# Windowed linear attention behind three convolutions: masks that read a copy of the scores, and norms and divisions set some steps apart

## The chip, the core and the metric

The kernel runs on one core of a Trainium2 chip. Its engines work beside each other, each in the order of its own queue: TensorE (PE), VectorE (DVE), ScalarE (ACT), GpSimd (POOL), and SyncE (SP), which issues most transfers. They wait for each other on semaphores. The metric is the device time of one execution in microseconds; less is better.

## The reference

Four layers act on x of shape 4 x 256 x 48 x 48 in float32. Each adds the result of its block, fed with a group-normalised x, to x:

```python
x = x + L0(_gn(x))   # 7x7 dilated convolution, softmax over 49 taps, applied to x
x = x + L1(_gn(x))   # 3x3 convolution, signs of weights
x = x + L2(_gn(x))   # 3x3 convolution, ternary weights
x = x + L3(_gn(x))   # attention, below
```

The change lies in layer 3 alone. It has 8 heads of 32 channels and three square windows, of the height divided by 1, 2 and 4:

```python
q, k = sigmoid(Wq x), sigmoid(Wk x);  v = Wv x / norm(Wv x)
for w in (1, 2, 4):
    wkv = box sum of k v^T over the window of side H // w around each pixel
    wk  = box sum of k over the same window
    attn = (q . wkv) / (q . wk + 1e-6)
out = Wout concat(attn of the three windows) + bout
```

A window is cut off at the edges of the image. The box sum is linear, so q . wkv is the sum over all pixels in the window of (q . k) v; the kernel computes it so.

## The kernel before

Layers 0 to 2 come first, image by image, and end near 1770 us of the profile. What follows is layer 3.

**Blocks and steps.** A block is one image b, one half ct of the channels (4 heads), and one band rb of 8 query rows: 4 x 2 x 6 = 48 blocks in that order. Inside it the loop runs over key tiles (a, c): 8 rows (band a) by 16 columns (c = 0, 1, 2), which are 128 keys and fill the partitions. `tiles_of` lists the key tiles that the widest window (half side 24) reaches, the nearest bands mixed with the farther ones. That makes 720 steps in all. In a step two pairs of heads are worked on, so that there are 1440 score tiles.

**One step**, in the order of the code:

- `scores`: for each of the two pairs, two matmuls of PE (L1159) write q . k for 128 keys and up to 8 x 48 queries into a PSUM tile `s`. Pool `ps_s` holds two of them, one for each pair, so PE can write the scores of the next step only when those of this step have been read.
- `masked`: the score tile is multiplied by the 0/1 mask of each window into SBUF tiles `sm0`, `sm1`, `sm2` (windows of half side 24, 12 and 6), of which six each are held, three steps' worth.
- `sums`: matmuls (L1237) multiply the masked scores of two steps ago (`LAG = 2`) by v and add them up in three PSUM accumulators.
- `background`: at most one job of other work.

**The masks before.** For a near tile (a band at most two from the queries' band, 1152 of the score tiles) the widest window covers all rows and the middle columns f0 to f1 fully. ACT copies that middle to `sm0` (L1193). DVE multiplies the remaining columns, one or two edges, from PSUM into `sm0`, and the whole of window 1 from PSUM into `sm1` (both L1216). For the nearest bands, at most one away, POOL[...] multiplies window 2 from ACT's copy into `sm2` (L1213, 768 of them). For a far tile (288) DVE multiplies the whole tile from PSUM. A score tile is thus read by ACT and by DVE before PE may write it again.

**Background.** `late` holds jobs with the step at which they are due; if none is due, the next job of `soon` runs. `soon` holds the projections of the next image (q, k, v, and the running sums of k for the box sums, whose rows POOL adds, L952), and the norms q . wk of each band. `norms` yields seven jobs: loads, POOL's subtraction (L1052) and product (L1056) for either half of the channels, `contract` (PE, L1063, sums over a head's channels) and `invert` (DVE). When the second half of a band is done, `finish` puts four jobs into `late`, 1, 4, 8 and 10 steps on: two divisions, of which each loads the reciprocal norms `rc` (L1286, four transfers) and multiplies (DVE, L1292), the first also loading the other half `o` and the residual `res`, and two output projections (PE, L1298).

**Who sets the order.** The matmuls of PE are kept in program order. For the other instructions a scheduler may move one ahead of another on its queue, within their dependencies.

Of the kernel before, what the change touches and what calls it, by code (L numbers as in the profile page):

```python
# [10 lines left out]
F32 = mybir.dt.float32  # L11
# [8 lines left out]
P = 128  # L20
# [4 lines left out]
RB = 8  # L25
# [93 lines left out]
def conv_preact_kernel(  # L119
# [692 lines left out]
    with (  # L812
# [199 lines left out]
        def norms(b, rb):  # L1012


            t = {}

            def load(ct):
                chans = slice(ct * P, (ct + 1) * P)
                t[ct] = hi = scr.tile([P, NW, RB, W], F32, tag="nhi", name="nhi")
                t["lo"] = lo = scr.tile([P, NW, RB, W], F32, tag="nlo", name="nlo", bufs=1)  # L1020
                t["q"] = qf = scr.tile([P, RB, W], F32, tag="nq", name="nq", bufs=1)
                nc.sync.dma_start(
                    out=qf.rearrange("p r w -> p (r w)"),
                    in_=qf_d[b][chans, rb * NB : (rb + 1) * NB],
                )
                for wi, h in enumerate(HALVES):

                    y0 = rb * RB + h - 1
                    n = max(0, min(RB, H - y0))
                    if n > 0:  # L1030
                        nc.sync.dma_start(
                            out=hi[:, wi, 0:n], in_=kb_d[b][wi, chans, y0 : y0 + n, :]
                        )
                    if n < RB:
                        nc.sync.dma_start(
                            out=hi[:, wi, n:RB],
                            in_=kb_d[b][wi, chans, H - 1 : H, :].to_broadcast([P, RB - n, W]),
                        )

                    y0 = rb * RB - h - 1  # L1040
                    n = min(RB, max(0, -y0))
                    if n < RB:
                        nc.sync.dma_start(
                            out=lo[:, wi, n:RB], in_=kb_d[b][wi, chans, y0 + n : y0 + RB, :]
                        )

            def subtract(ct):
                for wi, h in enumerate(HALVES):
                    n = min(RB, max(0, h + 1 - rb * RB))
                    if n < RB:  # L1050
                        hi = t[ct][:, wi, n:RB]
                        nc.gpsimd.tensor_sub(hi, hi, t["lo"][:, wi, n:RB])  # L1052

            def multiply(ct):
                for wi in range(NW):
                    nc.gpsimd.tensor_mul(t[ct][:, wi], t[ct][:, wi], t["q"])  # L1056

            def contract():
                ps = ps_m.tile([P, 512], F32, tag="st", name="norm_ps")
                for ct in range(NCT):  # L1060
                    for wi in range(NW):
                        tc.keep_in_program_order(
                            nc.tensor.matmul(  # L1063
                                ps[D * wi : D * (wi + 1), 0:NB],
                                head_sel[:, ct, :],
                                t[ct][:, wi].rearrange("p r w -> p (r w)"),
                                start=(ct == 0),
                                stop=(ct == NCT - 1),
                            )
                        )  # L1070
                ns = scr.tile([D * NW, NB], F32, tag="ns", name="ns", bufs=1)
                nc.scalar.copy(ns, ps[0 : D * NW, 0:NB])
                for wi in range(NW):
                    nc.sync.dma_start(
                        out=n_d[b][rb, :, wi, :], in_=ns[D * wi : D * wi + HEADS]
                    )

            def invert():
                nn = HEADS * NW * NB // P
                nr = scr.tile([P, nn], F32, tag="nr", name="nr")  # L1080
                flat = [d[b][rb].rearrange("h w n -> (h w n)") for d in (n_d, r_d)]
                nc.sync.dma_start(out=nr, in_=flat[0].rearrange("(p n) -> p n", n=nn))
                nc.vector.tensor_scalar_add(nr, nr, ATTN_EPS)
                nc.vector.reciprocal(nr, nr)
                nc.sync.dma_start(out=flat[1].rearrange("(p n) -> p n", n=nn), in_=nr)

            def between():
                multiply(0)
                load(1)

            return [
                lambda: load(0),
                lambda: subtract(0),
                between,
                lambda: subtract(1),
                lambda: multiply(1),
                contract,
                invert,
            ]
# [29 lines left out]
        def rows_seen(wi, a, rb):  # L1129

            h = HALVES[wi]
            return (
                max(0, a * RB - h + 1 - rb * RB),
                min(RB, a * RB + RB + h - rb * RB),
            )
# [5 lines left out]
        class Block:  # L1141
# [29 lines left out]
            def masked(self, a, c, s):  # L1171

                rb = self.rb
                sr, sc = rows_seen(0, a, rb)[0], cols_seen(0, c)[0]
                res = {}
                copied = None
                for wi in (0, 1, 2):
                    if not seen(wi, a, rb):
                        continue
                    r0, r1 = rows_seen(wi, a, rb)  # L1180
                    c0, c1 = cols_seen(wi, c)
                    n = r1 - r0
                    h = HALVES[wi]
                    sm = smp.tile(
                        [P, 2, RB, min(W, KC + 2 * h)], F32, tag=f"sm{wi}", name=f"sm{wi}"
                    )
                    res[wi] = sm[:, :, 0:n, 0 : c1 - c0]
                    mr = rb * RB + r0 - (a * RB - h + 1)
                    pieces = [(c0, c1)]
                    if wi == 0 and abs(a - rb) * RB + RB <= h:  # L1190

                        f0, f1 = max(0, c * KC + KC - h), min(W, c * KC + h + 1)
                        nc.scalar.copy(  # L1193
                            sm[:, :, 0:n, f0 - c0 : f1 - c0],
                            s[:, :, r0 - sr : r1 - sr, f0 - sc : f1 - sc],
                        )
                        copied = sm, r0, c0, f0, f1
                        pieces = [(c0, f0), (f1, c1)]
                    for p0, p1 in pieces:
                        if p0 == p1:  # L1200
                            continue
                        dst = sm[:, :, 0:n, p0 - c0 : p1 - c0]
                        mc = p0 - (c * KC - MCOL0[wi])
                        m = (
                            mask[wi][:, mr : mr + n, mc : mc + p1 - p0]
                            .unsqueeze(1)
                            .to_broadcast([P, 2, n, p1 - p0])
                        )
                        if wi == NW - 1 and copied and copied[3] <= p0 and p1 <= copied[4]:

                            big, br, bc = copied[:3]
                            src = big[:, :, r0 - br : r1 - br, p0 - bc : p1 - bc]
                            nc.gpsimd.tensor_mul(dst, src, m)  # L1213
                        else:
                            src = s[:, :, r0 - sr : r1 - sr, p0 - sc : p1 - sc]
                            nc.vector.tensor_mul(dst, src, m)  # L1216
                return res

            def begin(self):
                self.accs = [  # L1220
# [47 lines left out]
        def finish(b, rb, stage):  # L1268
# [1 line left out]

            t = {1: stage}

            def divide(ct):
                if ct == 0:
                    t[0] = op.tile([P, NW, NB], F32, tag="o", name="o", bufs=1)
                    nc.sync.dma_start(out=t[0].rearrange("p w n -> p (w n)"), in_=o_d[b][rb])
# [4 lines left out]
                            "(ct p) r w -> p ct r w", p=P  # L1281
                        ),
                    )
                rc = op.tile([P, NW, NB], F32, tag="rc", name="rc", bufs=1)
                for g in range(HG):
                    nc.sync.dma_start(  # L1286
                        out=rc[g * D : (g + 1) * D].rearrange("p w n -> p (w n)"),
# [1 line left out]
                        .rearrange("w n -> (w n)")  # L1289
                        .partition_broadcast(D),  # L1290
                    )
                nc.vector.tensor_mul(t[ct], t[ct], rc)  # L1292

            def out_proj(mo):
                ps = ps_m.tile([P, 512], F32, tag="st", name="out_ps")[:, 0:NB]
# [20 lines left out]
                    )  # L1316

            return [
                lambda: divide(0),
                lambda: divide(1),  # L1320
                lambda: out_proj(0),
                lambda: out_proj(1),
# [45 lines left out]
        def done(i):  # L1368

            b, ct, rb = order[i]  # L1370
            block = blocks.pop(i)
            if ct == 0:
                nc.sync.dma_start(out=o_d[b][rb], in_=block.stage.rearrange("p w n -> p (w n)"))
            else:
                for n, job in zip((1, 4, 8, 10), finish(b, rb, block.stage)):
                    late.append((step + n, job))
            nb, nct = b + (ct + 1) // NCT, (ct + 1) % NCT
            if nb < B:
                for a in LOADS.get(rb, ()):
                    while projected[nb] <= a:  # L1380
                        next_job()
                    load_kv(nb, nct, a)
# [72 lines left out]
```

## Time and profile before

| what | value |
|---|---|
| median of 3 runs (lowest, highest) | 4208.48 us (4205.66, 4213.35) |
| the profiled execution | 4190.68 us, span of its instructions 4188.9 us |
| PE, DVE busy in the span | 3524.6 us, 2265.2 us |
| ACT, POOL busy in the span | 985.1 us, 1217.2 us |
| layer 3 in the span | from about 1770 us to the end, 2419 us |
| masks of DVE, L1216 | 1256.5 us in 2976 instructions |
| window-2 masks of POOL, L1213 | 619.1 us in 768 |
| copies of ACT, L1193 | 598.3 us in 1152 |

A group of instructions is read so: line, engine, operation, tiles written <- tiles read, shape, count | busy time in us, mean ns of one | idle time of the engine just before them, and what ended it. Where a group mixes shapes, a view by form gives each shape its own row. A row of the waits reads: who waited <- for whom: us in all, times, longest.

### The profile page before, as it was taken

The page shows a single profiled execution, that of the slowest core. Times are in us where ns is not written, and L with a number is a line of the kernel's source. Part 1 is how long each engine was busy: PE and PEld are TensorE (multiplying, and loading weights), DVE is VectorE, ACT ScalarE, POOL GpSimd, SP SyncE. Part 2 cuts the span into 40 slices and gives each one's busy share as a digit, 9 for nine tenths or more (in the row PEclk, how much of TensorE's full clock was granted, in tenths as well). Part 3 has the DMA queues.
Part 4 walks back from the last instruction along what each step waited for, and adds up shares of the span by engine and source line. Part 5 has one row for each costly group of instructions (what it writes and reads, how often), then busy time and mean ns, then how long its engine had stood idle before and what let it go on. Part 6 is the DMA issues. An engine that isn't in the chain of part 4 may idle for free.

```text
span 4188.9 us, 65475 instructions
## 1 busy us (share of the span) xinstructions
PE 3524.6 (84%) x25060; PEld 2237.7 (53%) x25060; DVE 2265.2 (54%) x5022; ACT 985.1 (24%) x1915; POOL 1217.2 (29%) x1712
## 2 busy tenths in 40 slices
PE   5999998999899696388888878788978778988888
PEld 4777786787769574134444444434444434444444
DVE  7643234324331225356776667656667656667665
ACT  0101001100110202233332234323234323233332
POOL 0000000010000013465555345562245562223322
PEclk9999999999999798699999999999999999999999
DMA  7333015112500405654455454462353362331321
GB/s 272 131 58 71 23 72 65 42 36 81 72 27 32 37 1 193 177 138 137 150 166 144 114 158 135 126 159 80 93 165 129 124 159 76 93 107 48 93 65 54
DMA packets 366136, 430.06 MB, mean 103 GB/s; under 512 B 141667, under 2 KB 328835, under 8 KB 363395
## 3 DMA queue, kind: packets, MB, share of 16 engines
q1 hardware_dynamic: 360163, 416.37, 36.3%
q10 hardware_dynamic: 5520, 8.00, 0.6%
q8 instruction: 201, 3.29, 0.3%
q0 software_dynamic: 144, 1.52, 0.2%
q14 instruction: 108, 0.88, 0.1%
HBM read 293.12 MB, written 134.17 MB: 102 GB/s over the span
## 4 chain that ended last, share of the span: by engine, by line
PE 57%; DVE 14%; POOL 10%; DMA 9%; issue 4%; ACT 3%; SPq 2%; DVEq 0%; ACTq 0%; POOLq 0%
PE cv L504 15%; PE cv L639 11%; PE acc L1237 11%; PE s L1159 9%; DVE sm L1216 8%; PE out_ps L1298 5%; POOL pt L952 4%; ACT sm L1193 2%; PE proj_ps L898 2%; POOL nhi L1056 2%; PE ap L616 2%; DMA band_d<-e 1%; POOL nhi L1052 1%; POOL sm L1213 1%; DMA ks<-k_d 1%
## 5 line engine op out<-in xcount | busy, mean ns | idle before, releaser
L1216 DVE TENSOR_TENSOR sm<-s,masks 128x128 f32<-128x128 f32 (+14 forms) x2976 | 1256.5, 477 | 506.1 <-ACT sm L1193 487.5
L1159 PE MATMUL s<-qs,ks 128*128 128x320 f32 (+3 forms) x2880 | 798.4, 375 | 361.6 <-DVE sm L1216 257.2
L1213 POOL TENSOR_TENSOR sm<-sm,masks 128x336 f32<-128x336 f32 (+8 forms) x768 | 619.1, 821 | 1148.2 <-ACT sm L1193 1145.0
L1237 PE MATMUL acc<-sm,vs 128*32 128x384 f32 (+18 forms) x13440 | 894.7, 392 | 4.6 <-POOL sm L1213 4.6
L1193 ACT COPY sm<-s 128x528 f32<-128x528 f32 (+2 forms) x1152 | 598.3, 535 | 1196.9 <-PE s L1159 1047.5
L1159 PEld LDWEIGHTS s<-qs,ks 128*128 128x128 f32 x2880 | 460.8, 196 | 768.4 <-issue 449.4
L504 PE MATMUL cv<-v,wt 128*128 128x288 f32 x2912 | 761.9, 416 | 30.5 <-DVE v L460 21.6
L504 PEld LDWEIGHTS cv<-v,wt 128*128 128x128 f32 x2912 | 546.3, 191 | 195.7 <-issue 20.7
L1237 PEld LDWEIGHTS acc<-sm,vs 128*32 128x32 f32 x13440 | 358.4, 112 | 370.9 <-issue 229.7
L639 PE MATMUL cv<-pad,wl_sb 128*128 128x384 f32 (+1 forms) x2592 | 473.6, 345 | 17.1 <-ACT pad L710 12.1
L639 PEld LDWEIGHTS cv<-pad,wl_sb 128*128 128x128 f32 x1728 | 322.1, 193 | 17.6 <-issue 12.4
L448 POOL MEMSET v<- 128x192 f32 x28 | 8.3, 297 | 789.2 <-issue 422.4
L518 DVE SCALAR_TENSOR_TENSOR rows<-cv,rows 128x288 f32<-128x288 f32 x144 | 57.1, 451 | 284.2 <-PE cv L504 284.2
L952 POOL TENSOR_TENSOR pt<-pt 128x144 f32<-128x144 f32 x336 | 190.4, 567 | 59.5 <-DVE pt L948 36.6
L1056 POOL TENSOR_TENSOR nhi<-nhi,nq 128x384 f32<-128x384 f32 x144 | 146.6, 1022 | 21.4 <-DMA nhi<-kb_d 7.3
L672 DVE SCALAR_TENSOR_TENSOR x<-cv,alpha,x 128x384 f32<-128x384 f32 x48 | 29.7, 618 | 224.1 <-PE cv L639 224.0
L1298 PE MATMUL out_ps<-stage,wout_sb 128*128 128x384 f32 x288 | 121.9, 506 | 24.7 <-DVE stage L1292 24.7
L170 ACT ACTIVATE rsq_s<-gn_v 128x2 f32<-128x2 f32 x16 | 3.3, 204 | 557.7 <-DVE gn_v L197 557.6
L1298 PE MATMUL out_ps<-o,wout_sb 128*128 128x384 f32 x288 | 124.2, 514 | 10.0 <-ACT kp L920 5.7
L1307 DVE SCALAR_TENSOR_TENSOR res<-out_ps,bout_sb,res 128x384 f32<-128x384 f32 x48 | 29.7, 618 | 171.7 <-PE out_ps L1298 169.0
L972 PE MATMUL proj_ps<-wv_sb,xn 128*128 128x256 f32 x288 | 98.2, 472 | 25.8 <-ACT kp L920 13.5
L639 PEld LDWEIGHTS <-wl_sb 128*128 128x128 bf16 x864 | 84.8, 99 | 63.1 <-issue 4.4
(160 smaller groups left out, 2654.0 us busy)
## 6 DMA issues: line engine op xcount, KB each, us to landing
qs<-q_d SPq DMA_DIRECT2D x192, 192.0 KB
ks<-k_d SPq DMA_DIRECT2D x192, 192.0 KB
wt<-wt SPq DMA_DIRECT2D x80, 448.0 KB
kb_d<-pt SPq DMA_DIRECT2D x48, 576.0 KB
rc<-r_d SPq DMA_DIRECT2D x192, 144.0 KB
nhi<-kb_d SPq DMA_DIRECT2D x120, 192.0 KB
q_d<-hl SPq DMA_DIRECT2D x48, 384.0 KB
k_d<-hl SPq DMA_DIRECT2D x48, 384.0 KB
```

The lines of the kernel that those rows point to most:

```text
L504: nc.tensor.matmul(pss[half], wt[:, ct, k, :], vt[:, ct, :, t0 : t0 + NTH, k : k + HP], start=((part, ct, k) == (0, 0, 0)), stop=((part, c ...
L616: nc.tensor.matmul(pf[:, f, a:e], xTs[k + i][:n, f, mo * P : (mo + 1) * P], seen[:n, 1 + i, a:e], start=(i == 0), stop=(i == near[-1]),)
L639: nc.tensor.matmul(ps, w_sb[:, ct, t, mo * P : (mo + 1) * P], pad[:, ct, r0 : r0 + RB, c0 : c0 + W], start=(n == 0), stop=(n == len(parts) ...
L952: nc.gpsimd.tensor_add(pt[:, :, r, :], pt[:, :, r, :], up)
L972: nc.tensor.matmul(ps, xn[:, ct, c, :], proj["v"][:, ct, :], start=(ct == 0), stop=(ct == NCT - 1),)
L1056: nc.gpsimd.tensor_mul(t[ct][:, wi], t[ct][:, wi], t["q"])
L1159: nc.tensor.matmul(s[:, j, 0 : (r1 - r0) * (c1 - c0)], kvs[self.b, self.ct, a][0][:, 2 * pr + j, c, :], self.qs[:, 2 * pr + j, r0:r1, c0:c ...
L1193: nc.scalar.copy(sm[:, :, 0:n, f0 - c0 : f1 - c0], s[:, :, r0 - sr : r1 - sr, f0 - sc : f1 - sc],)
L1213: nc.gpsimd.tensor_mul(dst, src, m)
L1216: nc.vector.tensor_mul(dst, src, m)
L1237: nc.tensor.matmul(acc[D * j : D * (j + 1)].rearrange("p (r w) -> p r w", w=W)[:, r0:r1, c0:c1], kvs[self.b, self.ct, a][1][:, c, j, :], s ...
L1298: nc.tensor.matmul(ps, wout_sb[:, kt, mo * P : (mo + 1) * P], t[kt % NCT][:, kt // NCT, :], start=(kt == 0), stop=(kt == NW * NCT - 1),)
```

## The change

ACT copies the whole score tile of a near tile into `sm0`, 640 or 768 elements for each partition in place of 384, 400 or 528. POOL's window 2 and DVE's window 1 are multiplied from that copy, and then DVE multiplies the edges of `sm0` in place. The far tiles stay as they are. Two empty jobs stand between the last product of `norms` and `contract`. `finish` is cut into five jobs, at steps 1, 3, 5, 8 and 10: the loads come two steps ahead of the multiplication that needs them.

```diff
@@ norms
                 lambda: multiply(1),
+                lambda: None,
+                lambda: None,
                 contract,
@@ masked (the new body; tiles, view and times_mask only name slices)
-                    if wi == 0 and abs(a - rb) * RB + RB <= h:
-                        f0, f1 = max(0, c * KC + KC - h), min(W, c * KC + h + 1)
-                        nc.scalar.copy(
-                            sm[:, :, 0:n, f0 - c0 : f1 - c0],
-                            s[:, :, r0 - sr : r1 - sr, f0 - sc : f1 - sc],
-                        )
-                        copied = sm, r0, c0, f0, f1
-                        pieces = [(c0, f0), (f1, c1)]
...
-                        if wi == NW - 1 and copied and copied[3] <= p0 and p1 <= copied[4]:
-                            big, br, bc = copied[:3]
-                            src = big[:, :, r0 - br : r1 - br, p0 - bc : p1 - bc]
-                            nc.gpsimd.tensor_mul(dst, src, m)
-                        else:
-                            src = s[:, :, r0 - sr : r1 - sr, p0 - sc : p1 - sc]
-                            nc.vector.tensor_mul(dst, src, m)
+                if abs(a - rb) * RB + RB > HALVES[0]:
+                    times_mask(nc.vector, 0, (r0, r1), (c0, c1), s)
+                else:
+                    nc.scalar.copy(view(0, (r0, r1), (c0, c1)), s)
+                    for wi in range(NW - 1, 0, -1):
+                        if wi in tiles:
+                            rows, cols = rows_seen(wi, a, rb), cols_seen(wi, c)
+                            times_mask(
+                                nc.gpsimd if wi == NW - 1 else nc.vector,
+                                wi,
+                                rows,
+                                cols,
+                                view(0, rows, cols),
+                            )
+                    f0, f1 = max(0, c * KC + KC - HALVES[0]), min(W, c * KC + HALVES[0] + 1)
+                    for p0, p1 in ((c0, f0), (f1, c1)):
+                        if p0 < p1:
+                            here = view(0, (r0, r1), (p0, p1))
+                            times_mask(nc.vector, 0, (r0, r1), (p0, p1), here)
@@ finish
-            def divide(ct):
+            def load(ct):
                 if ct == 0:
...
-                nc.vector.tensor_mul(t[ct], t[ct], rc)
+            def divide(ct):
+                nc.vector.tensor_mul(t[ct], t[ct], t["rc"])
+
+            def between():
+                divide(0)
+                load(1)
...
-                lambda: divide(0),
+                lambda: load(0),
+                between,
                 lambda: divide(1),
@@ done
-                for n, job in zip((1, 4, 8, 10), finish(b, rb, block.stage)):
+                for n, job in zip((1, 3, 5, 8, 10), finish(b, rb, block.stage)):
```

In the changed kernel the masks of DVE and POOL stand at L1196, the copy at L1207, the scores at L1161, the sums at L1246, the division at L1303 and its loads of `rc` at L1295.

More of the change, by code (lines that the diff above doesn't have):

```diff
@@ L1173, in masked @@
                 rb = self.rb
[L1174 to L1184, printed above, removed]
+                (r0, r1), (c0, c1) = rows_seen(0, a, rb), cols_seen(0, c)
@@ L1185, in masked @@
+                tiles = {
+                    wi: smp.tile(
                         [P, 2, RB, min(W, KC + 2 * h)], F32, tag=f"sm{wi}", name=f"sm{wi}"
                     )
-                    res[wi] = sm[:, :, 0:n, 0 : c1 - c0]
-                    mr = rb * RB + r0 - (a * RB - h + 1)
-                    pieces = [(c0, c1)]
-                    if wi == 0 and abs(a - rb) * RB + RB <= h:
-                        f0, f1 = max(0, c * KC + KC - h), min(W, c * KC + h + 1)
-                        nc.scalar.copy(
-                            sm[:, :, 0:n, f0 - c0 : f1 - c0],
-                            s[:, :, r0 - sr : r1 - sr, f0 - sc : f1 - sc],
-                        )
-                        copied = sm, r0, c0, f0, f1
-                        pieces = [(c0, f0), (f1, c1)]
@@ L1199, in masked @@
[L1199 to L1208, printed above, removed]
-                        if wi == NW - 1 and copied and copied[3] <= p0 and p1 <= copied[4]:
-                            big, br, bc = copied[:3]
-                            src = big[:, :, r0 - br : r1 - br, p0 - bc : p1 - bc]
-                            nc.gpsimd.tensor_mul(dst, src, m)
-                        else:
-                            src = s[:, :, r0 - sr : r1 - sr, p0 - sc : p1 - sc]
-                            nc.vector.tensor_mul(dst, src, m)
@@ L1217, in masked, with view, times_mask @@
-                return res
+                    for wi, h in enumerate(HALVES)
+                    if seen(wi, a, rb)
+                }
+                def view(wi, rows, cols):
+                    (y0, _), (x0, _) = rows_seen(wi, a, rb), cols_seen(wi, c)
+                    return tiles[wi][
+                        :, :, rows[0] - y0 : rows[1] - y0, cols[0] - x0 : cols[1] - x0
+                    ]
+                def times_mask(engine, wi, rows, cols, src):
+                    mr = rb * RB + rows[0] - (a * RB - HALVES[wi] + 1)
+                    mc = cols[0] - (c * KC - MCOL0[wi])
+                    nr, ncol = rows[1] - rows[0], cols[1] - cols[0]
+                    m = mask[wi][:, mr : mr + nr, mc : mc + ncol]
+                    engine.tensor_mul(
+                        view(wi, rows, cols),
+                        src,
+                        m.unsqueeze(1).to_broadcast([P, 2, nr, ncol]),
+                    )
@@ new lines, in masked @@
+                if abs(a - rb) * RB + RB > HALVES[0]:
[11 more added lines that the diff above has]
+                                view(0, rows, cols),
+                            )
+                    f0, f1 = max(0, c * KC + KC - HALVES[0]), min(W, c * KC + HALVES[0] + 1)
[3 more added lines that the diff above has]
+                            times_mask(nc.vector, 0, (r0, r1), (p0, p1), here)
@@ L1219, in begin @@
+                return {
+                    wi: view(wi, rows_seen(wi, a, rb), cols_seen(wi, c)) for wi in tiles
+                }
             def begin(self):
@@ L1283, in divide @@
                     )
-                rc = op.tile([P, NW, NB], F32, tag="rc", name="rc", bufs=1)
+                t["rc"] = rc = op.tile([P, NW, NB], F32, tag="rc", name="rc", bufs=1)
                 for g in range(HG):
```

## The prediction

> **What bounds the kernel now.** I read the page from the top: busy shares, then the groups of the third layer, then the waits and the windows of that layer's stretch (1770 us to the end), and last single instructions in the timeline. The three convolution layers before it are untouched by the change. In the page's busy shares and costliest groups:
>
> ```profile
> PE 3524.6 (84%) x25060; PEld 2237.7 (53%) x25060; DVE 2265.2 (54%) x5022; ACT 985.1 (24%) x1915; POOL 1217.2 (29%) x1712
> ...
> L1216 DVE TENSOR_TENSOR sm<-s,masks 128x128 f32<-128x128 f32 (+14 forms) x2976 | 1256.5, 477 | 506.1 <-ACT sm L1193 487.5
> L1159 PE MATMUL s<-qs,ks 128*128 128x320 f32 (+3 forms) x2880 | 798.4, 375 | 361.6 <-DVE sm L1216 257.2
> L1213 POOL TENSOR_TENSOR sm<-sm,masks 128x336 f32<-128x336 f32 (+8 forms) x768 | 619.1, 821 | 1148.2 <-ACT sm L1193 1145.0
> ...
> L1193 ACT COPY sm<-s 128x528 f32<-128x528 f32 (+2 forms) x1152 | 598.3, 535 | 1196.9 <-PE s L1159 1047.5
> ```
>
> Attention is a ring: PE writes scores, ACT copies the middle, DVE masks, and PE's next scores wait for DVE to free the score buffer (257.2 us). DVE in turn is idle for 487.5 us until ACT's copy. The waits of PE and DVE in the attention stretch:
>
> ```profile
> PE s L1159 <- DVE sm L1216: 257.2, 355, 5.7
> PE norm_ps L1063 <- POOL nhi L1056: 40.7, 33, 4.8
> PE out_ps L1298 <- DVE stage L1292: 24.7, 8, 6.4
> ...
> DVE sm L1216 <- ACT sm L1193: 487.5, 503, 29.6
> DVE res L1307 <- PE out_ps L1298: 169.0, 46, 5.7
> DVE ss L983 <- POOL sq L982: 85.0, 35, 5.0
> ```
>
> Windows (columns: length, PE, PEld, DVE, ACT, POOL busy, clock, DMA) show two regimes. The first three are stretches full of background work (projections and norms), the fourth one without:
>
> ```profile
> 1860.00:2323.00 463.00, 378.60 (x3196) 195.40 (x3193) 315.79 (x700) 161.14 (x319) 252.79 (x339) 0.93 0.51 148
> 2466.00:2724.00 258.00, 202.88 (x1688) 108.19 (x1686) 183.68 (x413) 99.33 (x196) 138.40 (x202) 0.91 0.42 134
> ...
> 3097.00:3355.00 258.00, 203.07 (x1687) 108.34 (x1685) 182.06 (x408) 99.51 (x196) 137.68 (x202) 0.91 0.40 131
> ...
> 3757.00:3908.00 151.00, 135.68 (x1440) 68.67 (x1438) 110.14 (x264) 57.85 (x116) 50.28 (x67) 1.00 0.22 61
> ```
>
> In the quiet one PE is 90% busy and sets the pace. In the busy ones PE is at 79%, DVE at 71%, POOL at 54%: there DVE nearly sets it. In 2466:2724 DVE is idle 74 us; its waits there for anything but ACT's copies (POOL's squares 24.9, a store of pt 9.2, ACT 7.4 and small ones) come to 46, so only 28 us are slack.
>
> [...] All 2976 masks of L1216 read s from PSUM, and their by-form means, from 286 ns at 128 columns to 953 at 768, lie on one line, though POOL works beside them. L948, which reads cs twice from SBUF, is stretched (min/median/max in ns):
>
> ```profile
> L948 DVE TENSOR_TENSOR pt<-cs x144: 540/552/1383, 1612.5 to 3337.5; 128x384 f32<-128x384 f32 x144
> ```
>
> and the timeline shows why (start, length):
>
> ```profile
> 2524.08 2.82 DVE L948 TENSOR_TENSOR pt<-cs 128x384 f32<-128x384 f32 x3
> ...
> 2524.29 1.06 POOL L1213 TENSOR_TENSOR sm<-sm,masks 128x352 f32<-128x352 f32 x1 [4.73 <-ACT sm L1193]
> ...
> 2525.52 0.97 POOL L1213 TENSOR_TENSOR sm<-sm,masks 128x352 f32<-128x352 f32 x1 [0.17 <-ACT sm L1193]
> ...
> 2526.83 1.77 DVE L1216 TENSOR_TENSOR sm<-s,masks 128x240 f32<-128x240 f32 x4
> ```
>
> Three L948 take 2.82 us where three free ones would take 3 x 0.552 less overlaps. The second and third take 1.22 us each, both ending 0.42 us after a POOL product. The other way, an L1213 of 220 columns takes 0.61 us free and 1.52 behind an L1292. [...] from start to start, L948 takes 468 ns for 384 columns, L1216 514 ns for 432, both 0.96 columns per ns plus 66 ns. I take no gain from the source. [...] the copies of 400 and 528 columns (509 and 615 ns) give 0.83.
>
> **The change, part by part.**
>
> *Copies.* 384 grow from 528 to 768 columns, 768 from 384 or 400 to 640. At 0.83 ns: 814 and 708 ns, so 384 x 0.814 + 768 x 0.708 = 856 us against 598. The 258 us lie on an engine with over 1400 us idle in the stretch; each adds 0.2-0.3 us before masks and POOL, which the lag of two steps between scores and sums covers. Price alone 0; if the cover is gone, it shows as PE waiting for L1207 of the new kernel.
>
> *Release of scores.* 1152 of 1440 score buffers are freed by ACT's copy alone, no longer after DVE. The 288 far tiles are still masked from PSUM. So most of the 257.2 us goes, and what is late next is the masked tile: PE's sums on DVE.
>
> *Masks.* 2688 of the 2976 (all but the far forms: 96 of 815, 96 of 734, 48 of 953, 48 of 853 ns, 230 us) now have both inputs in SBUF, so 1027 us of DVE work join the contention with POOL. The holding part of a POOL product is its length less what it does ahead of reading: free 0.608, it ended 0.46 us after the DVE instruction that held it, so 0.15 us less. In 2466:2724: 138.4 - 202 x 0.15 = 108 us of holding. DVE must do 184 + 46 = 230. If a share f of the holding stops DVE, less 5.5 us already suffered (30 L948 at 652 against 552, 20 L925 at 673 against 549), DVE needs 230 + 108 f - 5.5. Masks and POOL's product start from the same copy and collide by design, but DVE also has work that doesn't collide[...]. I choose f = 0.5: 278 us, +20 on 258. f = 0.3 gives 257, no loss; f = 0.75 gives 305, +47. The busy windows are 979 us in all, 3.8 times this one: **+78 us (0 to +180)**.
>
> In the quiet window nearly each POOL product is a mask that collides: f = 0.75 of 50.3 - 67 x 0.15 = 40 gives DVE 110 + 30 = 140, POOL's holding in full 150, of 151. PE needs 136. The gain of the freed ring and the new limit about cancel: **0, from -4% to +3% of the remaining 1440 us, -58 to +43**.
>
> *Edges in place.* An edge follows the window-1 mask of the same tile and must wait for its end: in the built order 398 edges stand right behind it. Six masks at 3766.99 take 2.28 us where their lengths sum to 2.70: neighbours overlap by 0.083, which such a pair loses. 398 x 0.1 = 40 us on DVE, a third in busy windows: **+13 (0 to +40)**.
>
> *Norms and divisions.* The two empty steps give POOL's products two steps (some 6 us) before PE's contraction: PE's 40.7 us can go. Dividing two steps after its loads takes DVE's 21.4 us of waits for rc and PE's 24.7 + 3.5. No instruction or DMA is added; the same 10 loads per block row go into SP's queue, the first six two steps ahead of the product, the four of the second half behind the first product, which still frees their buffer. SP waits 98.6 us at L1286 for DVE today; that stays, and what sits behind it (loads of q, k, xr) is issued several steps before its use. The 24 + 48 background slots push norms into later blocks; they are ready long before their division. Of 69 us PE waits, some fall where DVE now limits: **-25 (-55 to 0)**.
>
> Sum: 78 + 0 + 13 - 25 = +66. Profiled span 4188.9 (execution 4190.7) becomes 4255 (4257); the median of the runs shown is 18 above that execution: 4208.5 + 66 = **4274**.
>
> **Rivals.** *A: the freed ring wins.* If f is under 0.3, because POOL slips into DVE's 487.5 us of idle, busy windows lose nothing, and a quarter to a half of the 257 us returns, plus the 25: -90 to -150, **about 4090**, faster. For it: that idle. Against: the idle lies in the quiet windows, where DVE must stay behind PE. It decides at f = 0.3. *B: full alternation.* POOL is held as well, its squares and norms come late, DVE waits for them: f = 0.75 in busy windows and all of the holding in quiet ones: 180 + 43 + 40 = +263, **4470**. Against: long stretches of DVE work that doesn't collide. *C: nothing*: gains and losses cancel within 8 us, **4208**; the sum has no reason to.
>
> **Numbers.** Main case 0.65 (own range 4217 to 4360), A 0.19, B 0.10, C 0.06. The range 4170 to 4390 takes in C, the weak end of A and the main case's unknown costs. A measurement of this kernel can tell 0.2% (8 us) from no change. Faster 0.19, same 0.06, slower 0.75.
>
> **What would show it.** Right: the mask rows of 448, 432 and 240 columns scatter widely above today's 614, 598 and 402 ns; POOL's products grow above 821 ns mean; PE's scores wait little for DVE, its sums (L1246) wait for DVE and POOL instead; the busy windows lengthen, the quiet ones don't. L1063 and L1303 lose their waits. Wrong: mask rows as short as today (no contention), or busy windows shorter.

## The result, and the profile after

The changed kernel takes **4356.62 us** (median of 4 runs, 4353.48 to 4363.11). The kernel before, run beside it, takes 4207.07 us. The ratio is **1.0356 [1.0338, 1.0374]**: 150 us slower, where 66 were forecast. The direction was right and the time lies inside the stated range, but the loss is more than twice the one forecast.

The profiled execution (4363.11 us, span 4361.3) is 172 us above that of before. Of these, 15 lie in layers 0 to 2, which the change doesn't touch: their end falls between 1769 and 1806 us in the profiles used here, and the profile before has the earliest. Layer 3, from its first matmul of scores on, went from 2420 to 2577 us. PE's busy time takes 102 of these 157 us, its idle time the other 55. Busy shares and the costliest groups of the kernel after:

```profile
PE 3633.6 (83%) x25060; PEld 2291.5 (53%) x25060; DVE 2737.3 (63%) x5022; ACT 1178.6 (27%) x1915; POOL 1484.9 (34%) x1712
...
L1196 DVE TENSOR_TENSOR sm<-sm,masks 128x624 f32<-128x624 f32 (+11 forms) x2688 | 1502.8, 612 | 226.2 <-ACT sm L1207 176.3
L1196 POOL TENSOR_TENSOR sm<-sm,masks 128x336 f32<-128x336 f32 (+8 forms) x768 | 801.9, 1062 | 1029.8 <-ACT sm L1207 1026.0
L1246 PE MATMUL acc<-sm,vs 128*32 128x384 f32 (+17 forms) x13440 | 1034.5, 401 | 92.5 <-DVE sm L1196 57.0
L1207 ACT COPY sm<-s 128x640 f32<-128x640 f32 (+1 forms) x1152 | 797.3, 733 | 1111.8 <-PE s L1161 687.8
L1161 PE MATMUL s<-qs,ks 128*128 128x320 f32 (+3 forms) x2880 | 750.4, 375 | 267.1 <-DVE sm L1196 183.6
...
L1196 DVE TENSOR_TENSOR sm<-s,masks 128x560 f32<-128x560 f32 (+3 forms) x288 | 224.3, 811 | 48.1 <-PE s L1161 47.4
```

The same 2976 masks on DVE, now two groups, take 1502.8 + 224.3 = 1727 us instead of 1256.5, and POOL's 768 products 801.9 instead of 619.1. PE's scores still wait 183.6 us for DVE. The forms tell which masks grew (DVE; the mean ns of one is the second figure after the bar). Two rows of the kernel before, then those after:

```profile
L1216 DVE TENSOR_TENSOR sm<-s,masks 128x624 f32<-128x624 f32 x256 | 204.2, 798 | 0.0
...
L1216 DVE TENSOR_TENSOR sm<-s,masks 128x128 f32<-128x128 f32 x384 | 109.6, 286 | 172.8 <-ACT sm L1193 171.9
```

```profile
L1196 DVE TENSOR_TENSOR sm<-sm,masks 128x624 f32<-128x624 f32 x256 | 257.9, 1037 | 60.8 <-ACT sm L1207 59.8
...
L1196 DVE TENSOR_TENSOR sm<-sm,masks 128x128 f32<-128x128 f32 x384 | 193.5, 504 | 11.2 <-PE s L1161 0.5
L1196 DVE TENSOR_TENSOR sm<-sm,masks 128x448 f32<-128x448 f32 x256 | 190.5, 766 | 25.0 <-ACT sm L1207 24.5
...
L1196 DVE TENSOR_TENSOR sm<-s,masks 128x640 f32<-128x640 f32 x96 | 75.0, 812 | 22.4 <-PE s L1161 22.2
```

The masks with two SBUF inputs went from 798 to 1037 ns (624 columns), from 286 to 504 (128) and from 614 to 766 (448). The far mask of 640 columns, still read from PSUM (`sm<-s`), stands at 812 ns, as before (815). One stretch of the timeline (start, length) shows both things that this document is about:

```profile
3945.42 1.38 DVE L1196 TENSOR_TENSOR sm<-s,masks 128x560 f32<-128x560 f32 x2
...
3946.21 1.26 PE L1161 MATMUL s<-qs,ks 128*128 128x384 f32 x4 [1.04 <-DVE sm L1196]
...
3946.86 1.50 ACT L1207 COPY sm<-s 128x768 f32<-128x768 f32 x2 [3.54 <-PE s L1161]
...
3947.69 3.39 DVE L1196 TENSOR_TENSOR sm<-sm,masks 128x624 f32<-128x624 f32 x3 [0.89 <-ACT sm L1207]
3947.74 3.20 POOL L1196 TENSOR_TENSOR sm<-sm,masks 128x432 f32<-128x432 f32 x2 [3.23 <-ACT sm L1207]
```

*Alternation.* The last two lines overlap throughout. The three masks (624, 624 and 128 columns) took 0.81, 1.63 and 1.11 us. Free, by the lengths of before, they are 0.80, 0.80 and 0.29: the second and third ended 0.67 and 0.15 us after a POOL product did, little more than their columns take at 0.96 per ns (0.65 and 0.13). Until then they stood still. *A far tile.* PE waits 1.04 us until DVE has read a far tile, then ACT copies the next tile, and DVE, by then out of work, waits 0.89 us for that copy.

The waits of PE and then of DVE in layer 3 of the kernel after (us in all, times, longest):

```profile
PE s L1161 <- DVE sm L1196: 183.6, 145, 9.1
PE acc L1246 <- DVE sm L1196: 57.0, 82, 2.5
...
PE norm_ps L1063 <- POOL nhi L1056: 49.9, 30, 6.9
...
PE acc L1246 <- POOL sm L1196: 33.1, 18, 4.6
```

```profile
DVE sm L1196 <- ACT sm L1207: 176.3, 137, 28.6
...
DVE stage L1303 <- DMA rc<-r_d: 36.1, 8, 5.6
```

PE's scores wait less often (145 times for 355) but longer (up to 9.1 us for 5.7), and the sums, which hardly waited before, now wait 57.0 + 33.1 us.

The quiet window is the same four blocks (last image, first half of the channels, bands 2 to 5) in both kernels: first before, then after (length, then busy PE, PEld, DVE, ACT, POOL, the granted clock, DMA share, GB/s):

```profile
3757.10:3907.80 150.70, 135.38 (x1439) 68.59 (x1438) 109.94 (x263) 57.72 (x115) 50.08 (x67) 1.00 0.22 60
```

```profile
3907.80:4067.90 160.10, 142.74 (x1439) 74.05 (x1438) 142.57 (x266) 74.85 (x116) 63.41 (x66) 0.97 0.20 53
```

DVE has 32.6 us more to do, and the window is 9.4 us longer. PE's own busy time takes 7.4 of the 9.4; its granted clock, full before, was half for 10.2 us of the window after.

### The profile page after: what moved, and what is told of

It reads as the page before. It is cut to its first block, busy times and chain, and to the rows that moved or that the text cites. A ratio compares the mean times of both kernels' runs of the same rounds, so it can differ in the third digit from the quotient of the medians.

```text
span 4361.3 us, 65425 instructions
## 1 busy us (share of the span) xinstructions
PE 3633.6 (83%) x25060; PEld 2291.5 (53%) x25060; DVE 2737.3 (63%) x5022; ACT 1178.6 (27%) x1915; POOL 1484.9 (34%) x1712
## 4 chain that ended last, share of the span: by engine, by line
PE 48%; DVE 22%; POOL 9%; issue 8%; DMA 8%; ACT 2%; SPq 2%; DVEq 0%; ACTq 0%; POOLq 0%
DVE sm L1196 15%; PE cv L504 14%; PE cv L639 11%; PE acc L1246 8%; PE s L1161 6%; POOL pt L952 5%; PE out_ps L1313 4%; PE ap L616 2%; DMA band_d<-e 1%; ACT sm L1207 1%; POOL nhi L1056 1%; DMA rows<-band_d 1%; POOL sm L1196 1%; POOL nhi L1052 1%; DVE pt L948 1%
## 5 line engine op out<-in xcount | busy, mean ns | idle before, releaser
L1196 DVE TENSOR_TENSOR sm<-sm,masks 128x624 f32<-128x624 f32 (+11 forms) x2688 | 1502.8, 612 | 226.2 <-ACT sm L1207 176.3
L1196 POOL TENSOR_TENSOR sm<-sm,masks 128x336 f32<-128x336 f32 (+8 forms) x768 | 801.9, 1062 | 1029.8 <-ACT sm L1207 1026.0
L1246 PE MATMUL acc<-sm,vs 128*32 128x384 f32 (+17 forms) x13440 | 1034.5, 401 | 92.5 <-DVE sm L1196 57.0
L1207 ACT COPY sm<-s 128x640 f32<-128x640 f32 (+1 forms) x1152 | 797.3, 733 | 1111.8 <-PE s L1161 687.8
L1161 PE MATMUL s<-qs,ks 128*128 128x320 f32 (+3 forms) x2880 | 750.4, 375 | 267.1 <-DVE sm L1196 183.6
L1161 PEld LDWEIGHTS s<-qs,ks 128*128 128x128 f32 x2880 | 473.5, 199 | 606.0 <-DVE sm L1196 302.0
L1246 PEld LDWEIGHTS acc<-sm,vs 128*32 128x32 f32 x13440 | 387.1, 113 | 579.8 <-DVE sm L1196 209.9
L639 PE MATMUL cv<-pad,wl_sb 128*128 128x384 f32 (+1 forms) x2592 | 473.7, 345 | 17.4 <-ACT pad L710 12.1
L1196 DVE TENSOR_TENSOR sm<-s,masks 128x560 f32<-128x560 f32 (+3 forms) x288 | 224.3, 811 | 48.1 <-PE s L1161 47.4
L952 POOL TENSOR_TENSOR pt<-pt 128x144 f32<-128x144 f32 x336 | 216.6, 645 | 40.7 <-DVE pt L948 13.3
L1052 POOL TENSOR_TENSOR nhi<-nhi,nlo 128x384 f32<-128x384 f32 (+3 forms) x112 | 121.9, 1089 | 65.6 <-DMA nlo<-kb_d 46.0
L616 PEld LDWEIGHTS ap<-seen,xT 120*128 120x128 f32 (+2 forms) x832 | 113.6, 217 | 13.3 <-ACT seen L609 11.0
```

The lines of the kernel that those rows point to most:

```text
L616: nc.tensor.matmul(pf[:, f, a:e], xTs[k + i][:n, f, mo * P : (mo + 1) * P], seen[:n, 1 + i, a:e], start=(i == 0), stop=(i == near[-1]),)
L639: nc.tensor.matmul(ps, w_sb[:, ct, t, mo * P : (mo + 1) * P], pad[:, ct, r0 : r0 + RB, c0 : c0 + W], start=(n == 0), stop=(n == len(parts) ...
L952: nc.gpsimd.tensor_add(pt[:, :, r, :], pt[:, :, r, :], up)
L1161: nc.tensor.matmul(s[:, j, 0 : (r1 - r0) * (c1 - c0)], kvs[self.b, self.ct, a][0][:, 2 * pr + j, c, :], self.qs[:, 2 * pr + j, r0:r1, c0:c ...
L1196: engine.tensor_mul(view(wi, rows, cols), src, m.unsqueeze(1).to_broadcast([P, 2, nr, ncol]),)
L1207: nc.scalar.copy(view(0, (r0, r1), (c0, c1)), s)
```

## The experiments

The theory was the prediction's: DVE's and POOL's products, all with two SBUF inputs now, hold each other, and that costs more than the freed score buffers return. The rivals were the longer copies, the edges that follow window 1 in place, and the far tiles that keep the ring closed. Each ratio and median stands against the kernel before in the same set of runs, whose median was 4207.73 us beside masks_alone, steps_alone, copy_whole and edges_late, 4211.76 beside before_nopool, after_nopool, far_copy and window1_first, and 4214.33 beside after_twice, before_twice, after_dve2 and hybrid. Differences from the kernel before are taken from the ratio where it and the medians part by a few us.

### The two halves of the change

*masks_alone*: the new `masked`, with the norms and `finish` of before.

```diff
-                lambda: None,
-                lambda: None,
                 contract,
...
-    for n, job in zip((1, 3, 5, 8, 10), finish(b, rb, block.stage)):
+    for n, job in zip((1, 4, 8, 10), finish(b, rb, block.stage)):
```

> The changed masks with the norms and divisions of the kernel before. Theory (DVE is held by POOL wherever both read SBUF, 464 us of stretched masks in the changed kernel, and DVE then sets the pace in quiet and busy windows alike): nearly the whole loss of 150 us, 4330 to 4390 us. Rival (the two empty steps push the norms into the second half of an image, where DVE and POOL then collide): under 4280 us.

*steps_alone*: the kernel before, with the two empty steps and the five jobs.

```diff
+                lambda: None,
+                lambda: None,
                 contract,
...
-    for n, job in zip((1, 4, 8, 10), finish(b, rb, block.stage)):
+    for n, job in zip((1, 3, 5, 8, 10), finish(b, rb, block.stage)):
```

> The empty steps in the norms and the five jobs of the divisions, with the masks of the kernel before. Theory: a small gain or nothing, 4170 to 4215 us, since some 70 us of PE's waits stand there. Rival (the moved norms make the loss): over 4260 us.

Measured: masks alone 4372.22 us, ratio 1.0393 [1.0358, 1.0427], +165 us; steps alone 4194.36 us, 0.9959 [0.9945, 0.9973], -17 us by the ratio (-13 by the medians). 1.0393 x 0.9959 = 1.0350, which is the whole change: the halves add up. The whole loss is in the masks. Steps alone is the only kernel here that does the whole work and beats the one before. Its waits, though, are not those that the prediction said would go:

```profile
PE norm_ps L1063 <- POOL nhi L1056: 35.0, 22, 5.5
...
DVE stage L1296 <- DMA rc<-r_d: 28.0, 7, 5.9
```

The norms' wait fell from 40.7 to 35.0 only, and DVE's waits for `rc` rose from 21.4 in all to the 28.0 shown. With the new masks the empty steps do more: PE waits 82.9 us for the norms in masks alone, 49.9 in the whole change.

### The longer copies by themselves

*copy_whole*: the kernel before, with ACT copying the whole tile; DVE masks from PSUM as before and overwrites what it needs.

```diff
                         nc.scalar.copy(
-                            sm[:, :, 0:n, f0 - c0 : f1 - c0],
-                            s[:, :, r0 - sr : r1 - sr, f0 - sc : f1 - sc],
+                            sm[:, :, 0:n, 0 : c1 - c0],
+                            s[:, :, r0 - sr : r1 - sr, c0 - sc : c1 - sc],
                         )
```

> The kernel before, but ACT copies the whole near tile; DVE still multiplies window 1 and the edges from PSUM, and frees the scores. Theory: ACT has room, 4205 to 4235 us. Rival (the copies, 0.2 us longer, delay masks and the release of the scores, and make most of the loss): over 4290 us.

Measured: 4277.73 us, 1.0167 [1.0133, 1.0202], +70 us, above what the theory expected and short of the rival. The longer copies show as a longer wait of DVE, and behind it of PE (487.5 and 257.2 before):

```profile
DVE sm L1216 <- ACT sm L1193: 555.4, 528, 31.6
```

```profile
PE s L1159 <- DVE sm L1216: 314.8, 517, 6.1
```

In the ring of before a copy lies between PE's scores and DVE's masks of the same buffer, and 0.2 us more of it (535 to 730 ns in the mean) comes round. The price 0 doesn't hold in that ring. In the new one, where the copy alone frees the buffer, no run varied it.

### The edges

*edges_late*: the changed kernel; DVE does both tiles' window 1 first and the edges after them, and keeps that order, so that no edge stands right behind its own window 1.

```diff
-                            times_mask(nc.vector, 0, (r0, r1), (p0, p1), here)
+                            edges.append((p0, p1))
...
@@ step
+                for _, do_edges in both:
+                    do_edges()
```

> The changed kernel with DVE's masks kept in program order, the edges of both pairs behind window 1 of both, so that no edge stands right behind the mask it must wait for (398 do in the changed kernel). Theory (being held by POOL is the cost): 4310 to 4360 us, at most 40 us gained. Rival (an edge that waits for the end of its window 1 loses 0.2 us, 80 us in all, on the engine that sets the pace): 4260 to 4300 us.

Measured: 4362.38 us, 1.0359 [1.0315, 1.0403]: no gain, and 2 us above the theory's range. The sums, which need the edges, now wait for DVE longer (57.0 us without this edit):

```profile
PE acc L1254 <- DVE sm L1196: 167.3, 156, 10.3
```

In the changed kernel 407 masks start 0.08 to 0.15 us after the mask before them ended, here 36. This shows only that the order doesn't pay; what the adjacent pairs lose is not separated from what the later edges cost.

### POOL's products left out

*before_nopool* and *after_nopool*: window 2 of the nearest tiles isn't multiplied; the sums read ACT's copy.

```diff
@@ before_nopool
-                            nc.gpsimd.tensor_mul(dst, src, m)
+                            res[wi] = src
@@ after_nopool
-                        if wi in tiles:
+                        if wi in tiles and wi < NW - 1:
...
-                    wi: view(wi, rows_seen(wi, a, rb), cols_seen(wi, c)) for wi in tiles
+                    wi: view(wi if wi < NW - 1 else 0, rows_seen(wi, a, rb), cols_seen(wi, c))
+                    for wi in tiles
```

> The kernel before without POOL's product for window 2: the sums of window 2 read ACT's copy unmasked, so that 768 products are left out. Theory (POOL's products stop nothing while DVE reads scores from PSUM): hardly faster, 4165 to 4207 us. Rival (POOL is near a limit before as well): under 4140 us.

> The changed kernel without POOL's product for window 2 (left out in the same way). Theory (DVE is held by POOL's own products above all, and the background holds it for the rest): most of the 150 us goes, 4200 to 4260 us, and stretched masks fall from 464 us to under 180. Rival 1 (the longer copies or the edges' waits make the loss): over 4310 us. Rival 2 (the freed score buffers are a real gain that the holding hid): under 4160 us, below the kernel before without those products.

Measured: 4144.14 us, 0.9846 [0.9813, 0.988], and 4052.06 us, 0.9635 [0.9609, 0.9661]. Without POOL's products the kernel with the old masks is 65 us shorter, the one with the new masks 304. Both lie below what the theory expected, before_nopool just above its rival's limit of 4140, after_nopool well under the 4160 of its second rival. Read the other way, with no product of POOL the new masks are 0.9635 / 0.9846 = 0.979 of the old ones, some 90 us *faster*. Part of that is the steps' 17. So the new masks, with their freed ring, are a real gain; it is POOL's products that turn it round. DVE's masks in after_nopool:

```profile
L1196 DVE TENSOR_TENSOR sm<-sm,masks 128x624 f32<-128x624 f32 (+11 forms) x2688 | 1191.7, 493 | 265.7 <-ACT sm L1207 218.5
```

493 ns, where the same group stands at 612 in the changed kernel. The holding that is left, 134 us in 304 masks, comes from POOL's norms, squares and running sums: each of the 304 ends some 15 ns plus its columns / 0.96 ns after one of these, where a mask of the kernel before takes columns / 0.96 + 150 ns in all (286 ns at 128 columns, 798 at 624).

### POOL's products done twice

*before_twice* and *after_twice*: the POOL product is issued twice, with the same result. The edit of after_twice, shortened; in before_twice the line of the product stands twice.

```diff
+                            for _ in range(2 if wi == NW - 1 else 1):
+                                times_mask(
+                                    nc.gpsimd if wi == NW - 1 else nc.vector,
...
```

> The changed kernel with every window-2 product of POOL done twice. Theory (each product's time is added to DVE's queue): leaving the products out gave 304 us, so doing them twice costs about as much again, 4600 to 4700 us. Rival (the first collision is what costs, POOL's length doesn't matter): 4360 to 4450 us.

> The kernel before with every window-2 product of POOL done twice. Theory (masks that read PSUM are not held): leaving them out gave 64 us, so 4250 to 4340 us, from POOL's queue alone, with DVE's masks as short as before. Rival (POOL's queue sets the pace in either kernel, and the masks' source doesn't matter): over 4450 us.

Measured: after_twice 4718.78 us, 1.122 [1.1191, 1.1249]; before_twice 4317.32 us, 1.0253 [1.0237, 1.027]; the first lies 19 us above the theory's range, the second inside it. The same added work costs some 360 us with masks that read the copy and 107 with masks that read PSUM. The masks of DVE, first in after_twice, then in before_twice:

```profile
L1196 DVE TENSOR_TENSOR sm<-sm,masks 128x624 f32<-128x624 f32 (+11 forms) x2688 | 1814.9, 728 | 217.9 <-ACT sm L1207 168.2
```

```profile
L1217 DVE TENSOR_TENSOR sm<-s,masks 128x128 f32<-128x128 f32 (+14 forms) x2976 | 1255.0, 476 | 557.4 <-ACT sm L1193 529.9
```

With POOL's window-2 products left out, once and twice, the masks take 493, 612 and 728 ns from SBUF, and 476, 477 and 476 ns from PSUM (the means from PSUM include the 288 far masks). Together these six kernels, at three amounts of POOL's work, show the cause: the masks from PSUM aren't touched by POOL, those from the copy grow in step with what POOL does.

### Window 2 on DVE

*after_dve2*: the changed kernel, all of its work, with window 2 on DVE too.

```diff
                             times_mask(
-                                nc.gpsimd if wi == NW - 1 else nc.vector,
+                                nc.vector,
...
```

> The changed kernel with window 2 multiplied by DVE from the copy, in place of POOL: nothing is left out, DVE does 768 products more (some 0.37 us each from start to start, 283 us), POOL none. Theory (the holding costs more than the products themselves): DVE's products fit into what the removed holding leaves, 4090 to 4200 us, under the kernel before. Rival (DVE is simply full, whoever does it): 4290 to 4380 us.

Measured: 4208.96 us, 1.0001 [0.9985, 1.0018]: 148 us below the changed kernel, even with the one before, and 9 us above the range of the theory.

```profile
L1196 DVE TENSOR_TENSOR sm<-sm,masks 128x256 f32<-128x256 f32 (+18 forms) x3456 | 1470.4, 487 | 166.3 <-ACT sm L1207 147.3
```

3456 + 288 masks on one engine keep DVE busy for 2658.4 us in the span. That is less than the 2737.3 of the changed kernel, in which POOL does 768 of them. Here a second engine that took turns with the first was worth less than nothing.

### The far tiles

*far_copy*: the changed kernel, in which ACT copies the 288 far tiles too and DVE masks them in place, so that every score buffer is freed by ACT.

```diff
-                    times_mask(nc.vector, 0, (r0, r1), (c0, c1), s)
+                    nc.scalar.copy(view(0, (r0, r1), (c0, c1)), s)
+                    whole = view(0, (r0, r1), (c0, c1))
+                    times_mask(nc.vector, 0, (r0, r1), (c0, c1), whole)
```

> The changed kernel, but ACT copies the 288 far tiles as well and DVE masks them in place, so that no score buffer waits for DVE. Theory (DVE's throughput under holding is the limit): PE's waits move from the scores to the sums and the time stays, 4340 to 4390 us. Rival (the far tiles are what keeps the freed ring from paying: PE waits there for a DVE that is far behind): 4250 to 4310 us.

Measured: 4330.57 us, 1.0287 [1.0258, 1.0317], some 28 us below the changed kernel, between theory and rival. PE's scores no longer wait for DVE at all, but its sums do:

```profile
PE acc L1248 <- DVE sm L1196: 122.7, 155, 5.8
...
PE acc L1248 <- POOL sm L1196: 64.9, 43, 5.1
```

The 183.6 us of waits at the scores are gone, the time fell by 28: most of these waits weren't caused by the far tiles as such. DVE is behind, and PE waits for it at the one place or at the other.

### Two attempts at a better version

*window1_first*: steps_alone with window 1 ahead of the edges, masks from PSUM.

```diff
...
-                for wi in (0, 1, 2):
+                for wi in (1, 0, 2):
...
```

> The kernel before with the empty steps and the five jobs of the divisions, and with DVE's window 1 ahead of the edges: window 1 reads PSUM and doesn't wait for ACT's copy, which the edges do. Theory (scores are held by DVE's wait for ACT's copy, 487 us of idle): the release comes up to 0.5 us earlier in near tiles, 4080 to 4170 us. Rival (DVE's order doesn't matter, its queue is full enough): 4180 to 4210 us like the steps alone.

Measured: 4224.76 us, 1.0032 [1.0014, 1.0049], missed by both: slower than steps_alone. The copy now stands behind DVE's window 1, though both only read the score tile:

```profile
ACT sm L1195 <- DVE sm L1218: 1244.7, 690, 47.0
```

*hybrid*: steps_alone in which only the tiles without window 2 are masked from a whole copy; those with it keep the middle copy and masks from PSUM. The edit is against the changed kernel.

```diff
-                    nc.scalar.copy(view(0, (r0, r1), (c0, c1)), s)
+                    near = NW - 1 in tiles
...
+                    nc.scalar.copy(
+                        view(0, (r0, r1), (g0, g1)), s[:, :, :, g0 - c0 : g1 - c0]
+                    )
...
```

> The changed kernel, but in the nearest tiles, which have a product of POOL, ACT copies the middle alone and DVE reads the scores from PSUM, as before; in the 384 tiles two bands away, which have none, DVE reads ACT's whole copy. Theory: DVE is held by the background alone and in a third of the near tiles, while their score buffers are freed early: 4140 to 4200 us. Rival (the whole copies cost as much as the release gains): 4200 to 4260 us.

Measured: 4211.19 us, 1.0000 [0.9988, 1.0012]: no gain on the kernel before, and slower than steps_alone, as the rival had it. The largest wait of PE is still the old one:

```profile
PE s L1161 <- DVE sm L1196: 244.3, 336, 6.4
```

It is 257.2 us in the kernel before: PE still waits for DVE nearly as long, though DVE no longer frees the farther of the near tiles.

## Why the prediction was half right

**Holding: right, in cause and in amount.** Summed over the trace, the time by which DVE's masks exceed their columns / 0.96 + 150 ns is nothing in the kernel before and about 462 us in 934 masks after. All 934 end columns / 0.96 + 8 to 22 ns after a POOL instruction has ended; for 647 it is a window-2 product, for the others POOL's background. The prediction's own terms were 54 us for the busy window x 3.8 = 205, and 30 us for 151 us of quiet time x 1440 = 286, together 491. By place it was near too. The busy windows can be found again in masks_alone, which has the same jobs at the same steps, by their first and last matmul of scores: 169 us of holding lie in them and 294 in the rest of layer 3. In the quiet window DVE was to have 140 us of work; it has 142.6.

**The quiet windows: "gain and new limit cancel", 0. This step failed.** Cut at the same matmuls, the busy windows of masks_alone are longer than before by 46 us (979 to 1026), where 78 + 13 were forecast, and the rest of layer 3 by 119 us (1441 to 1560), where 0 was forecast and 43 was the most. The sign that the prediction named, longer busy windows and unchanged quiet ones, came out the other way round in size. The argument was that DVE's 140 us fit into a window of 151, beside PE's 136. The work came as forecast, the fit did not: the four blocks take 160.1 us after, 6% more, where the range ended at 3%.

What that sum left out is time that neither engine uses. DVE is idle for 17.5 us of the 160.1: 6.3 in 51 gaps of 0.12 us, most of them edges that wait for their own window 1, and 11.2 in 15 longer gaps, 13 of them next to a far tile, as in the timeline: DVE's backlog delays PE's next scores, then DVE runs dry until PE and ACT have delivered. PE is idle for 17.4, of which 16.5 are waits for DVE at the scores (10.5 before). That POOL's products make this limit is shown: without them the same four blocks take 136.8 us (after_nopool), with them on DVE 147.5 (after_dve2). That the gaps do is argued only: without those behind window 1 nothing was gained (edges_late), with the far tiles' buffers freed 28 us in the whole kernel (far_copy). How the 9.4 us split between gaps and PE's lower clock is not shown either: the block in which the clock was halved for 10.2 us has 4.9 of the 9.4.

The last image shows gain and limit apart (both halves, from the first matmul of scores): 520 us before and 516 in before_nopool, 473 in after_nopool, 544 after. Without POOL's products the new masks are worth 43 us there; POOL's products cost 71 in the new form and 4 in the old one. The limit cost more than the gain, where the prediction let them cancel.

**"Most of the 257.2 us goes": failed.** 183.6 are left at the scores, and 90 came at the sums. The prediction named the next late thing, the masked tile, rightly. But it counted 1152 buffers of 1440 as freed and overlooked that the 288 others are spread between them, and that an engine that is late must be waited for somewhere (far_copy).

**Copies: price 0 not borne out.** Their lengths were right (801 and 698 ns measured for 814 and 708), the cover was not: +70 us in the old ring. What they cost in the new one was not tried by itself.

**Edges: +13, not refuted and not confirmed.** Their count was right (407 gaps for 398 pairs), their price too low: such a pair loses the 0.083 us of overlap and waits 0.12 us besides, 0.2 in all where 0.1 was used. But the order without these gaps brought nothing.

**Norms and divisions: -17 for -25.** The size is near; the mechanism is not the one given, as the waits for norms and `rc` stayed. With the old masks PE's scores wait 244.1 us for DVE instead of 257.2; but hybrid has 244.3 and gains nothing, so where the 17 us come from is open.

In sum, 66 = 91 - 25 became 150. The masks cost 165 us (46 in the busy windows for the 91, 119 in the rest for the 0), and the steps brought 17 for the 25; 165 - 17 = 148. The step that makes the difference is the rest, priced at 0.

**The rivals.** A, the freed ring wins, was true of the ring and lost to POOL: without POOL's products the new form is 92 us faster than the old (4144 to 4052), as A had it. B, full alternation, asked for f = 0.75 in busy windows; the 169 us held in 979, set against POOL's holding of 108 us in 258, make it 0.41, near the 0.5 chosen. C is out.

**Open.** PE's granted clock in layer 3 fell from 0.944 to 0.909: it was halved for 270 us before and for 468 after, and PE was busy in 223 and 348 of them. A matmul of the sums with 384 columns (L1246, after) took 490 ns on average at the full clock and 847 at the half. An estimate from these figures: 125 us more of busy PE at half the clock, at 1 - 490 / 847, cost it some 53 of the 102 us by which its busy time grew. The lower clock is thus a rival for part of the loss, or only went with it; no run parted the two. It doesn't order the kernels (in layer 3 after_nopool, at 0.937, is 159 us faster than the one before, and after_dve2, at 0.922, is even with it), and masks from PSUM are no longer at a low one (476 ns in before_twice, at 0.918).

## What to carry to other kernels

Before masks or products are moved from PSUM to a copy in SBUF in order to free a PSUM buffer, add up what GpSimd does in the same stretch: here 934 VectorE masks with two SBUF inputs stood still beside its instructions, for 462 us in all, and that turned a gain of some 90 us into a loss of 150. An engine that is to be busy for 140 of 151 us is not covered by the 11 left: count the gaps that it can't use before calling it a tie. When a ring of buffers is to be freed by another engine, look at the tiles that still go the old way: with one in five of them left, 183.6 of 257.2 us of the wait stayed. And look at whether the slow engine itself gets faster: with all of them freed, the wait moved to the sums and 28 us came back.

## What the hardware showed beside this

- A held DVE mask ends its columns / 0.96 + 15 ns after the POOL instruction that held it (0.67 us for 624 columns, 0.15 for 128 in the stretch above; within 7 ns of it for all 934 in the changed kernel): nearly its whole work comes after the wait.
- The source by itself made no visible difference: the 1754 masks of the changed kernel that read the copy and weren't held take columns / 0.96 + 150 ns, within 2 ns on average, as the 2976 from PSUM did before.
- POOL's products cost 65 us even where they hold no mask (before_nopool), more than PE's wait for them at the sums (4.6 us) suggests. Which way they do so stays open.
- Two engines that only read one PSUM tile, ACT and DVE, were run one after the other in the program as built: ACT waits 1244.7 us for DVE when DVE's read stands first in the code (window1_first).
